# A two-layer graph network on one core: layer 1's mean row out of unused mask columns, norms from LayerNorm's statistics, and a late last column for three tiles

## The chip, the cores and the metric

The kernel runs on one core of one Trainium2 chip. Its time is the device time of one execution in microseconds (us). Three runs of the kernel before gave 1134.03, 1134.79 and 1137.2 us; the median is 1134.79 us.

## The reference

Input: x of 2708 x 256 in fp32 and a sparse 0/1 matrix adj of 2708 x 2708. Two layers follow; each adds a graph attention and then a mixture of experts (top 2) to x. The change concerns the attention of layer 1, cut here to what matters:

```
x = LayerNorm(x)
Wx   = logmap0(x)[:, 1:] @ W_gcn            # logmap0: arccosh(x0) * y / |y|, y = x[:, 1:]
h    = logmap0(proj(expmap0([0, Wx]))) @ W_att
e    = h @ a1 + (h @ a2).T
att  = softmax(where(adj > 0, e, -9e15), axis=1)
emb  = proj(elu(att @ h));   out = expmap0(sigmoid(logmap0(emb)))
```

In a softmax over a row, h @ a1 cancels, so every neighbour j has the weight p_j = exp(h_j . a2), whatever the row: a row's result is the sum of p_j h_j over its neighbours, divided by the sum of p_j. A row without a neighbour gets the plain mean of all rows of h. The maps only scale rows: h_j is a matrix product u_j times a factor that depends on two norms, that of the normalised x_j and that of u_j.

## The kernel before

**Tiles.** Rows lie in T = 22 tiles: 0 to 19 of 128 rows, 20 and 21 of 74 each (TAIL); LAST is 21. D is 256. The order of instructions on TensorE (PE), DVE, ACT and SP is the order in which the program writes them; only POOL's is left to the framework. Each engine works in order.

**Layer 0** (attention, line 1246, and experts) lasts until about 662 us. Then a stage of layer 1 follows, in which a step counter (`Turns`) interleaves pairs of tiles: `prepare1` adds two partial sums (POOL), takes LayerNorm's statistics (DVE, line 434), the root on ACT (lines 441 and 442), and applies it (line 450); `project1` turns the rows (PE), copies them (ACT, line 1571), multiplies with w1x (PE, line 473) and evicts u_ps: ACT squares u with a sum into `norms` (line 1584) and copies u into h_all (line 1586). `square_rows` (line 1458) takes the norm of the normalised x on ACT too. Column 0 of each normalised row goes to `c0` (POOL).

**Factors.** `factors1(lo, n)` works on [128, n] statistics, one column a tile: a root of three blocks of norms (ACT Ln and Exp, lines 1603 and 1604, one Newton step on DVE), log1p as a series (about 20 DVE instructions), the scale of each row, p_all = exp(score) on ACT (line 1613) and p_scale = p_all * scale. It runs for 12 tiles, and after the projections for the other 10. `split_h` then writes p_j h_j of each tile as two fp32r halves, `half0` (ACT, line 1635) and the remainder `half1` (DVE, line 1636), with p_j itself in column D.

**Attention 1.** For a tile i of rows, `sum_up(i, j)` multiplies the mask block of (i, j), widened from fp8 to fp32r, with both halves of tile j: 22 x 2 matmuls of 128x258 (line 1649) sum in one PSUM bank. `widen(i, part)` casts the blocks of even or odd j, 128x1408, on POOL (line 1525) or ACT (line 1527) into one of four buffers. Rows without a neighbour get an artificial one: row 74 of tile LAST holds TINY/N times the sum of all h, at weight TINY. `add_h` makes that sum: 22 fp32 matmuls with scale as the weights (line 1656), from h_all; `split` then writes it into the halves (lines 1635 and 1636). Tiles 0 and 1 are summed first, over j from 0 to FIRST = 12; then come the mean and the rest of their columns; then tiles 2 to 21.

**After a tile**, `finish1`: DVE RECIPROCAL (line 1772), ACT Relu, Exp and Tanh (1775 to 1777), DVE twice (1779, and 1780 which reads PSUM), ACT Square (1784). When the last tile of a group is done (tiles 0 to 5, 6 to 11, 12 to 17, 18 to 21), `points1` of the group starts (line 1824): root and log chains on DVE and ACT, x1, LayerNorm, the logits on PE, `pick`, `rank` on PE, `number` on DVE, and the scatter of the rows to `rows_d` in DRAM, one indirect DMA a tile and choice, issued by POOL (line 681). Experts 1 works on blocks of 128 rows: SP fetches a block from rows_d (line 772) and its weights (lines 756 and 760), PE turns it (tr_ps, line 468), multiplies (lines 887 and 905), DVE weighs. Blocks 0 to 7 are known after groups 0 and 1, blocks 8 to 19 after group 2, the rest after group 3; `bias_ps` (line 858) and `number_ps` (826) belong to that planning.

**The order from tile 2 on** comes from a planner at build time, `Clock`: every piece of work is a generator that yields ("PE", 0.265) and the like, an engine and an assumed time in us, or a `Mark` to wait for; `Slots` are its buffers. It writes the instructions in the order in which the pieces would start. Its times are assumptions; on the chip each engine's queue then runs in that order. `widener` gives casts of tiles below 12 to POOL, later even parts to ACT.

The mask has no use for columns 74 to 127 of tiles 20 and 21: they are set to zero (lines 483 and 484), and the rows of PSUM that they make are not read.

Of the kernel before, what the change touches and what calls it, by code (L numbers as in the profile page):

```python
# [22 lines left out]
P = 128  # L23
# [123 lines left out]
def kernel(  # L147
# [260 lines left out]
    def log1p(u):  # L408

        t = ts(u, 1.0, OP.add)  # L410
        k = ts(t.bitcast(I32), 23, OP.logical_shift_right, dtype=I32)
        down = ts(k, -1.0, OP.mult, 254.0, OP.add, dtype=I32)
        scale = ts(down, 23, OP.logical_shift_left, dtype=I32).bitcast(F32)
        m = tt(tt(u, scale, OP.mult), ts(scale, -1.0, OP.add), OP.add)
        z = tt(m, recip(ts(m, 2.0, OP.add)), OP.mult)
        z2 = tt(z, z, OP.mult)
        terms = [2.0 / (2 * n + 1) for n in range(8)]
        q = ts(z2, terms[7], OP.mult)
        for c in reversed(terms[1:7]):
            q = sts(q, c, OP.add, z2, OP.mult)  # L420
        q = sts(q, terms[0], OP.add, z, OP.mult)
        return tt(ts(k, -127.0, OP.add, math.log(2.0), OP.mult), q, OP.add)

# [996 lines left out]
    ln_a1 = Norm("a1")  # L1420
    norms = kept("norms", 1.0, 2 * T).rearrange("p (k t) -> p k t", k=2)

# [32 lines left out]

    def square_rows(xp, pair):
        for q, (t, r) in enumerate(pair):
            nc.scalar.activation(row_tile("junk", 4)[:r, 1:], xp[q][:r, 1:], AF.Square,
                                 accum_out=norms[:r, 0, t:t + 1])

    def ahead(b):
# [13 lines left out]
        if left == 1:  # L1475
            rsqrt(ts(ln_a1.mv[:, :2 * AHEAD, 1], LN_EPS, OP.add), ln_a1.rstd[:, :2 * AHEAD])
            for k, pair in enumerate(pairs[:AHEAD]):
                keep_rows(h_all[:, 2 * k:2 * k + 2, :D], pair)
                if k < AHEAD - 1:
                    normed[k] = [(xn_tile if k < 2 else xr0_tile)()[:, :D] for _ in pair]  # L1480
                    for xp, (t, r) in zip(normed[k], pair):
                        ln_a1.apply(xp, x_all[:, t], t, r)
        if left == 0:
            for k, pair in enumerate(pairs[:AHEAD - 1]):
                square_rows(normed[k], pair)

# [24 lines left out]
    zeros = filled("zeros", 0.0, T, pool=att)  # L1511
    tiny = filled("tiny", TINY, pool=att)
    nc.scalar.preload_act_table_set(LN_TABLE)
    HALF = T // 2
# [14 lines left out]

    c0, scale, p_all, p_scale = kept("c0", 1.0), kept("scale"), kept("p_all"), kept("p_scale")  # L1530

    def xr_tile():
# [6 lines left out]
    def prepare1(pair):  # L1539

        xa = h_all[:, pair[0][0]:pair[0][0] + 2, :D]
        xb = [xr_tile()[:, :D] for _ in pair]
        fetch_rows(xa, sums0[0], pair)
        for q, (t, r) in enumerate(pair):
            fetch_row(xb[q], sums0[1], t, r)
        yield 3
        for q, (t, r) in enumerate(pair):
            nc.gpsimd.tensor_tensor(xa[:r, q], xa[:r, q], xb[q][:r], OP.add)
        yield 1
        keep_rows(xa, pair)  # L1550
        for q, (t, r) in enumerate(pair):
            ln_a1.stats(xa[:r, q], t, r)
        yield 1
        ln_a1.root(pair)
        yield 1
        ln_a1.mend(pair)
        xp = [xr_tile()[:, :D] for _ in pair]
        for q, (t, r) in enumerate(pair):
            ln_a1.apply(xp[q][:r], xa[:r, q], t, r)
        yield 1  # L1560
        yield from project1(pair, xp)

    def project1(pair, xp):
        ps = ps_tile("tr_ps", "tr").rearrange("p (t c n) -> p t c n", c=DC, n=P)
        for q, (t, r) in enumerate(pair):
            turn_rows(xp[q][:r], r, ps[:, q])
            nc.gpsimd.tensor_copy(c0[:r, t:t + 1], xp[q][:r, 0:1])
        yield 1
# [3 lines left out]
        else:  # L1572
            for q, (t, r) in enumerate(pair):
                nc.scalar.copy(xt[:, q, :, :r], ps[:, q, :, :r])
        if pairs.index(pair) >= AHEAD - 1:
            square_rows(xp, pair)
        yield 1
# [5 lines left out]
        for q, (t, r) in enumerate(pair):  # L1583
            nc.scalar.activation(row_tile("junk", 4)[:r, 1:], us[q][:r, :D - 1], AF.Square,
                                 accum_out=norms[:r, 1, t:t + 1])
            nc.scalar.copy(h_all[:r, t, :], us[q][:r, D - 1:])  # L1586

    def minus(v):

        nc.vector.tensor_scalar(v[..., 1:], v[..., :1].bitcast(F32), -1.0, None, op0=OP.mult)  # L1590

    def factors1(lo, n):

        hi = lo + n


        d = ts(c0[:, lo:hi], -1.0, OP.add, THETA_EPS, OP.max)
        v = stat(3 * n)
        sts(d, 2.0, OP.add, d, OP.mult, v[:, :n])
        nc.vector.tensor_scalar(v[:, n:].rearrange("p (k t) -> p k t", k=2), norms[:, :, lo:hi],  # L1600
                                MIN_NORM * MIN_NORM, None, op0=OP.max)
        y = stat(3 * n)
        nc.scalar.activation(y, v, AF.Ln)
        nc.scalar.activation(y, y, AF.Exp, scale=-0.5)
        yield 1
        y = newton(v, y)
        u = tt(tt(v[:, :n], y[:, :n], OP.mult), d, OP.add)
        f = tt(log1p(u), y[:, n:2 * n], OP.mult)
        wx = tt(tt(v[:, 2 * n:], y[:, 2 * n:], OP.mult), f, OP.mult)
        part = sts(wx, LEAST, OP.max, recip(ts(wx, MIN_NORM, OP.max)), OP.mult)  # L1610
        tt(part, f, OP.mult, scale[:, lo:hi])
        score = tt(scale[:, lo:hi], h_all[:, lo:hi, D], OP.mult)
        nc.scalar.activation(p_all[:, lo:hi], score, AF.Exp)
        yield 1

        tt(p_all[:, lo:hi], scale[:, lo:hi], OP.mult, p_scale[:, lo:hi])
# [25 lines left out]
    def sum_up(i, j):  # L1644
        k = rows_of(j)
        if i not in accs:
            accs[i] = ps_tile("att_ps", "acc")
        for half_k in halves:
            nc.tensor.matmul(accs[i][:, :D + 2], wide_masks[i, j % 2][:k, j // 2, :],  # L1649
                             half_k[:k, j, :], start=(j == 0 and half_k is halves[0]),  # L1650
                             stop=(j == LAST and half_k is halves[1]))

    def add_h(mean, lo, hi):

        for t, r in tiles[lo:hi]:
            nc.tensor.matmul(mean[:96, :D], scale[:r, t:t + 1].to_broadcast([r, 96]),
                             h_all[:r, t, :D], start=t == 0, stop=t == LAST)

    turns = Turns()
    FIRST = 12  # L1660
    last = pairs[AHEAD - 1]
    normed[AHEAD - 1] = [xr_tile()[:, :D] for _ in last]
    for xp, (t, r) in zip(normed[AHEAD - 1], last):
        ln_a1.apply(xp, x_all[:, t], t, r)
    for k in range(AHEAD):
        turns.start(project1(pairs[k], normed[k]), k)
    for k in range(17):
        if AHEAD + k < len(pairs):
            turns.start(prepare1(pairs[AHEAD + k]))
        turns.step()  # L1670
        if 6 <= k < 10:
            widen(k % 2, k < 8)

        if k == FIRST // 2 - AHEAD + 10:
            turns.start(factors1(0, FIRST))
        if k >= 14:
            lo = 4 * (k - 14)
            split_h(lo, lo + 4)
    split_h(lo + 4, FIRST)
    turns.start(factors1(FIRST, T - FIRST))  # L1680
    turns.finish()
    psum_stage(wide=5, acc=3)
    mean = ps_tile("mean_ps")
    for j in range(FIRST):
        for i in range(2):
            sum_up(i, j)
    add_h(mean, 0, T)
    split_h(FIRST, FIRST + 4)
    split_h(FIRST + 4, LAST)
    nc.scalar.preload_act_table_set(TANH_TABLE)  # L1690
    split(LAST, slice(64, 96), mean[64:96, :D], TINY / N)
    split(LAST, slice(0, TAIL), h_all[:TAIL, LAST, :D], p_scale[:TAIL, LAST:])
    for part in range(2):
        for t in range(FIRST + part, T, 2):
            for i in range(2):
                sum_up(i, t)
        widen(2, part)

# [19 lines left out]
    acc_slots = {t: acc.take() for t in range(2)}  # L1718
    wide_slots = {(2, part): wides.take() for part in range(2)}

    wide_at = {(i, part): Mark() for i in range(2, T) for part in range(2)}
    for part in range(2):
        wide_at[2, part].at = 0.0
    started, widened = Mark(), Mark()
# [12 lines left out]
    def widener():  # L1737
        for i in range(3, T):
            for part in range(2):
                wide_slots[i, part] = yield from wides.get()  # L1740
                clock.start(widen_one(i, part, wide_tile()), 0)
# [8 lines left out]
    def attention():  # L1750
        for i in range(2, T):
            acc_slots[i] = yield from acc.get()
            accs[i] = ps_tile("att_ps", "acc")
            for part in range(2):
                yield wide_at[i, part]
                for j in range(part, T, 2):
                    yield "PE", 0.265
                    sum_up(i, j)
                clock.set(wide_slots[i, part])
            clock.start(finish1(*tiles[i]), 0)  # L1760
        att_scope.close()
        late_pools()
        clock.set(started)

    def finish1(t, r):
# [253 lines left out]
    experts1.beside = add_beta  # L2019
    for t in range(2):  # L2020
        clock.start(finish1(*tiles[t]), 0)
    clock.start(widener())
# [55 lines left out]
```

## Time and profile before

| | |
|---|---|
| runs | 1134.03, 1134.79, 1137.2 us (median 1134.79) |
| the profiled execution | 1136.56 us, its span 1134.8 us, granted TensorE clock 0.958 |
| projections of layer 1 | TensorE 662.2 to 708.8 |
| attention 1, tiles 0 and 1, with the mean | 710.4 to 730.6 |
| attention 1, the other tiles | to 862.8 |
| wait before the first block of experts 1 | 867.8 to 880.05 |
| last matmul of experts 1 | about 1094 |

The profile is of one execution, and its times count from the span's start. The span is that of the profiled instructions; what lies around it makes the 1136.56 us. Each line of a timeline has a start, a duration, the engine, the source line, the operation, what it writes and reads, and in brackets the idle time before it with what ended it. Line numbers are those of the kernel before; after `log1p` and further changes, the changed kernel's are 16 to 125 higher.

### The profile page before, as it was taken

The numbers are of one execution on the slowest core, as the hardware profiler recorded it, in microseconds if no ns is written. First come the engines' busy times: TensorE is split into PE (matmuls) and PEld (weight loads), VectorE is DVE, ScalarE is ACT, GpSimd is POOL, SyncE is SP. The second block draws the span as 40 slices with busy tenths as digits, with TensorE's granted clock in tenths as the row PEclk, the third lists the DMA queues.
The fourth block names the chain that finished last, engine by engine and source line by source line (L and its number), as shares of the span: only waits on it lengthen the run. The fifth ranks groups of instructions, "written<-read, shape, count | busy, mean of one in ns | idle before, by whom it ended". The sixth has DMA issues, their size and how long they took to land. (4 is left out here: it accounts for less than half of the span.)

```text
span 1134.8 us, 21254 instructions
## 1 busy us (share of the span) xinstructions
PE 1023.5 (90%) x6665; PEld 909.0 (80%) x6665; DVE 541.9 (48%) x2083; ACT 572.7 (50%) x1599; POOL 367.1 (32%) x417
## 2 busy tenths in 40 slices
PE   5999999998999999999999999998984888999950
PEld 3788888886889999999998853898984787898840
DVE  7778888887420111111111235647777552122368
ACT  4867667664524444444443357536754543444320
POOL 7531112111242222212222350253345166433442
PEclk9999999999989999999999999999897889999985
DMA  9965354431889999999899959400225477787974
GB/s 289 288 242 177 136 175 156 166 95 58 303 251 295 327 326 322 323 306 321 257 311 335 340 160 278 150 1 6 76 84 153 124 215 188 187 213 178 282 194 133
DMA packets 165461, 238.96 MB, mean 211 GB/s; under 512 B 11035, under 2 KB 140374, under 8 KB 162632
## 3 DMA queue, kind: packets, MB, share of 16 engines
q1 hardware_dynamic: 146524, 214.09, 57.9%
q0 software_dynamic: 18816, 23.42, 10.6%
q8 instruction: 56, 0.92, 0.3%
q14 instruction: 65, 0.53, 0.2%
HBM read 205.54 MB, written 54.99 MB: 230 GB/s over the span
## 5 line engine op out<-in xcount | busy, mean ns | idle before, releaser
L911 DVE TENSOR_SCALAR yo<-out_ps,w 128x256 f32<-128x256 f32 x92 | 44.5, 483 | 402.4 <-PE out_ps L905 401.9
L1246 PE MATMUL att_ps<-g_all,z 128*128 128x257 f32 (+3 forms) x968 | 223.6, 383 | 0.0
L905 PE MATMUL out_ps<-room,ht 128*128 128x256 f32 x872 | 201.1, 383 | 0.0
L1246 PEld LDWEIGHTS att_ps<-g_all,z 128*128 128x128 f32 (+3 forms) x968 | 174.9, 186 | 29.6 <-issue 3.1
L887 PEld LDWEIGHTS hid_ps<-xt,room 128*128 128x128 f32 x1504 | 176.4, 193 | 7.3 <-issue 2.5
L887 PE MATMUL hid_ps<-xt,room 128*128 128x128 f32 x1504 | 177.7, 277 | 4.2 <-DMA room<-in_L_ffn_W_dram 3.7
L905 PEld LDWEIGHTS out_ps<-room,ht 128*128 128x128 f32 x872 | 162.7, 192 | 21.3
L1232 ACT ACTIVATE zr<-e_bc,minus_one,g_all 128x256 f32<-128x256 f32 (+3 forms) x242 | 130.4, 591 | 46.4 <-DVE z L1235 45.8
L916 POOL DMA_INDIRECT sums<-yo,xg x43 | 66.8, 1554 | 235.0 <-DVE side L879 173.4
L891 ACT ACTIVATE ht<-hid_ps,w_t 128x128 f32<-128x128 f32 x376 | 128.7, 364 | 28.0 <-PE hid_ps L887 8.8
L681 POOL DMA_INDIRECT rows_d<-xr,place x88 | 92.2, 1048 | 121.0 <-DVE xr L450 76.9
L1649 PE MATMUL att_ps<-half,wide_mask 128*128 128x258 f32 (+1 forms) x968 | 124.5, 290 | 2.5 <-ACT h_all L1586 1.5
L1649 PEld LDWEIGHTS att_ps<-half,wide_mask 128*128 128x128 f32 (+1 forms) x968 | 121.5, 195 | 3.9 <-ACT h_all L1586 2.4
L1235 DVE SCALAR_TENSOR_TENSOR z<-zr,mask_t 128x256 f32<-128x256 f32 (+3 forms) x242 | 96.9, 422 | 29.6 <-ACT zr L1232 18.3
L916 POOL DMA_INDIRECT sums<-yo,xr x45 | 70.6, 1569 | 118.0 <-DMA sums<-yo,xr 30.0
L891 ACT ACTIVATE ht<-hid_ps,w1x 128x128 f32<-128x128 f32 x180 | 62.4, 363 | 88.6 <-PE hid_ps L887 85.0
L881 ACT ACTIVATE w<-xg,side 128x1 f32<-128x1 f32 x43 | 12.7, 294 | 169.2 <-DVE side L879 169.2
L1525 POOL CAST wide_mask<-mask_t 128x1408 fp32r<-128x1408 fp8e4 x31 | 42.5, 1375 | 101.6 <-PE att_ps L1649 67.5
L887 PE MATMUL hid_ps<-lo,wide_mask 128*128 128x128 f32 x480 | 63.4, 287 | 5.6 <-DMA wide_mask<-in_L_ffn_w_dram 4.7
L887 PEld LDWEIGHTS hid_ps<-lo,wide_mask 128*128 128x128 f32 x480 | 60.6, 200 | 9.4 <-issue 6.5
L905 PE MATMUL out_ps<-wide_mask,ht 128*128 128x256 f32 x240 | 59.6, 393 | 0.0
L468 PE MATMUL tr_ps<-ident,xr 128*128 128x128 f32 (+1 forms) x214 | 38.2, 289 | 22.2 <-DMA xr<-rows_d 13.9
(292 smaller groups left out, 1325.0 us busy)
## 6 DMA issues: line engine op xcount, KB each, us to landing
room<-in_L_ffn_W_dram SPq DMA_DIRECT2D x94, 1024.0 KB
wide_mask<-in_L_ffn_w_dram SPq DMA_DIRECT2D x60, 512.0 KB
room<-in_adj_dram SPq DMA_DIRECT2D x20, 1354.0 KB
room<-in_L_ffn_w_dram SPq DMA_DIRECT2D x30, 512.0 KB
rows_d<-nobody SPq DMA_DIRECT2D x1, 7511.0 KB
rows_d<-nobody SPq DMA_DIRECT2D x5, 1295.0 KB
sums<-nobody SPq DMA_DIRECT2D x2, 2944.0 KB
xr<-rows_d SPq DMA_DIRECT2D x45, 129.5 KB
```

What stands on the lines that cost most here:

```text
L468: nc.tensor.transpose(ps[:, c, :r], src[:, c * P:(c + 1) * P], ident[:r, :r])
L681: ins = nc.gpsimd.indirect_dma_start(out=self.rows_d[:, :], in_=self.rows[t][:r], in_offset=None, out_offset=bass.IndirectOffsetOnAxis(ap= ...
L887: nc.tensor.matmul(ps[:, :P], w1_b[:, c, f * P:(f + 1) * P], xt[:, c, :], start=(c == 0), stop=(c == DC - 1))
L891: nc.scalar.activation(ht[:, f, :], ps[:, :P], self.func, bias=self.bias[:, f, b:b + 1])
L905: nc.tensor.matmul(ps[:, :D], ht[:, f, :], self.rooms[b % 3][1][:, f, :], start=False, stop=(f == self.FC - 1))
L911: nc.vector.tensor_scalar(yo, ps[:, :D], w, None, op0=OP.mult)
L916: ins = nc.gpsimd.indirect_dma_start(out=self.sums[k][:, :], in_=yo, in_offset=None, out_offset=bass.IndirectOffsetOnAxis(ap=self.rows.pop ...
L1232: nc.scalar.activation(zr[:k, :n], e_bc[:k, lo:lo + n], AF.Relu, bias=minus_one[:k], scale=g_all[:k, j, D + 1:D + 2])
L1235: nc.vector.scalar_tensor_tensor(z[:k, :n], zr[:k, :n], 1.0, mask_t[:k, j // 2, lo:lo + n, j % 2], op0=OP.add, op1=OP.mult)
L1246: nc.tensor.matmul(accs[i][:r, :D + 1], z[:k, q * P:q * P + r], g_all[:k, j, :D + 1], start=(j == 0), stop=(j == LAST))
L1525: nc.gpsimd.tensor_copy(m, src)
L1649: nc.tensor.matmul(accs[i][:, :D + 2], wide_masks[i, j % 2][:k, j // 2, :], half_k[:k, j, :], start=(j == 0 and half_k is halves[0]), stop ...
```

## The change

1. *Norms from statistics.* `square_rows` goes. `inward1` computes the squared norm of y from LayerNorm's variance, rstd and c0 (D * var * rstd^2 - c0^2), and the factor f of the first map for all 22 tiles at once, in `f_all`. `factors1` keeps the second map alone, for 16 and then 6 tiles. All are generators now, so that single steps can be placed between others; the copies to c0 move ahead of the turning.
2. *First casts.* The four casts for tiles 0 and 1 all go to POOL; two were on ACT.
3. *Order.* inward1 and the first factors run among the last projections, tiles 0 to 2 are split ahead of the last eviction, and two steps of the remaining factors follow each split of tiles 4 to 15.
4. *The mean.* `add_h` goes. Tile 20, now SPARE, is summed first after tiles 0 and 1. Columns 126 and 127 of its widened masks get 1/p_j, in two parts (`spare_columns`, six DVE instructions), so that rows 126 and 127 of its sum hold the sum of all h but that of LAST. ACT copies this sum to SBUF (`keep_total`); in the middle of tile 2's even columns two fp32 matmuls add those two rows and LAST's own part; `split_last` makes the halves of LAST. Only then do tiles 0, 1 and SPARE (OPEN) get their column LAST, between tile 2's even and odd columns, the masks for it kept by three small POOL copies; SPARE's sum is put back by a matmul with the identity, as its bank's sum was closed. Tile 2 sits in a bank of another pool ("wide").
5. *What the planner and the framework make of it.* The order of tiles is 0, 1, 20, 2, 3, ... 19, 21. finish1 of tile 20 moves from the end of the attention to its start. ACT casts (20, even); POOL casts (20, odd) and then those of tiles 2, 3 and so on. Six fetches of x_d for the last group move on SP ahead of one block's fetch and weight load.

The diff, cut to its core (`log1p` and `factors1` get a `yield` after nearly every instruction):

```diff
+    def inward1():
+        n = T
+        rest = tt(sts(ln_a1.mv[:, :, 1], float(D), OP.mult, ln_a1.rstd, OP.mult), ln_a1.rstd, OP.mult)
+        rest = tt(rest, tt(c0, c0, OP.mult), OP.subtract)
...
+        nc.vector.tensor_scalar(v[:, n:], rest, MIN_NORM * MIN_NORM, None, op0=OP.max)
+        y = yield from root_of(v)
...
+        log = yield from log1p(u)
+        yield
+        tt(log, y[:, n:], OP.mult, f_all)
...
         for half_k in halves:
-            nc.tensor.matmul(accs[i][:, :D + 2], wide_masks[i, j % 2][:k, j // 2, :],
+            late = j == LAST and i in OPEN
+            nc.tensor.matmul(accs[i][:, :D + 2],
+                             last_masks[i][:k] if late else wide_masks[i, j % 2][:k, j // 2, :],
...
-    def add_h(mean, lo, hi):
-        for t, r in tiles[lo:hi]:
-            nc.tensor.matmul(mean[:96, :D], scale[:r, t:t + 1].to_broadcast([r, 96]),
-                             h_all[:r, t, :D], start=t == 0, stop=t == LAST)
+    SPARE = TF
+    OPEN, NEXT = (0, 1, SPARE), 2
+    def spare_columns():
+        p_inv = ts(p_all, 1e-30, OP.max)
+        p_inv = recip(p_inv)
+        by_part = p_inv.rearrange("p (j s) -> p s j", s=2)
+        for part in range(2):
+            hi, lo = (wide_masks[SPARE, part][:, :, P - 2 + k] for k in range(2))
+            nc.vector.tensor_copy(hi, by_part[:, part])
+            nc.vector.tensor_tensor(lo, by_part[:, part], hi.bitcast(F32), OP.subtract)
...
-    FIRST = 12
+    FIRST, SOON = 16, 3
...
+        if k == 15:
+            go(near, 1)
+            go(near)
+            split_h(0, SOON)
...
         if 6 <= k < 10:
-            widen(k % 2, k < 8)
+            widen(k % 2, k < 8, pool=True)
...
+    far = factors1(FIRST, T - FIRST)
+    for t in range(SOON, FIRST):
+        split_h(t, t + 1)
+        if t >= SOON + 1:
+            go(far, 2)
+    go(far)
+    split_h(FIRST, LAST)
+    keep_last_masks()
     nc.scalar.preload_act_table_set(TANH_TABLE)
...
     for part in range(2):
-        for t in range(FIRST + part, T, 2):
+        for t in range(FIRST + part, LAST, 2):
             for i in range(2):
                 sum_up(i, t)
-        widen(2, part)
+        widen(SPARE, part)
+    spare_columns()
...
     def attention():
-        for i in range(2, T):
+        for i in order:
...
+                    if i == NEXT and part == 0 and j == 8:
+                        slot = yield from bank.get()
+                        ps = ps_tile("mean_ps")
+                        yield total_at
+                        yield "PE", 0.9
+                        nc.tensor.matmul(ps[:96, :D], two_last, total["tile"][:, :D], start=True, stop=False)
+                        nc.tensor.matmul(ps[:96, :D], scale[:TAIL, LAST:].to_broadcast([TAIL, 96]),
+                                         h_all[:TAIL, LAST, :D], start=False, stop=True)
+                        clock.start(split_last(ps, slot, last_at), 0)
...
+                if i == NEXT and part == 0:
+                    yield last_at
+                    for k in OPEN:
+                        if k == SPARE:
+                            yield "PE", 0.5
+                            nc.tensor.matmul(accs[k][:, :D + 2], ident, total["tile"], start=True,
+                                             stop=False)
+                            clock.set(total["slot"])
+                        yield "PE", 0.265
+                        sum_up(k, LAST)
+                        clock.start(finish1(*tiles[k]), 0)
...
+    def split_last(ps, slot, mark):
+        yield "ACT", 0.4
+        by = TINY / N
+        nc.scalar.activation(halves[0][64:96, LAST, :D], ps[64:96, :D], AF.Copy, scale=by)
+        yield "DVE", 0.5
+        nc.vector.scalar_tensor_tensor(halves[1][64:96, LAST, :D], ps[64:96, :D], by,
...
+        yield "ACT", 0.4
+        lo, by = slice(0, TAIL), p_scale[:TAIL, LAST:]
+        nc.scalar.activation(halves[0][lo, LAST, :D], h_all[lo, LAST, :D], AF.Copy, scale=by)
+        yield "DVE", 0.5
+        nc.vector.scalar_tensor_tensor(halves[1][lo, LAST, :D], h_all[lo, LAST, :D], by,
...
```

The last DVE instruction of `split_last` is at line 1885 of the changed kernel (N1885 in the prediction).

## The prediction

> **What bounds the kernel now.** I read, in this order: the page's first two parts, TensorE's timeline through layer 1's attention, its waits behind it, and then POOL's and DVE's timelines for what those waits hang on.
>
> ```profile
> span 1134.8 us, 21254 instructions
> PE 1023.5 (90%) x6665; PEld 909.0 (80%) x6665; DVE 541.9 (48%) x2083; ACT 572.7 (50%) x1599; POOL 367.1 (32%) x417
> ```
>
> TensorE is busy 90%, but shares say nothing of one stage. The stage of the change, on TensorE's timeline (start, duration, work, and in brackets the idle time before with what ended it):
>
> ```profile
> 706.90 1.94 PE L473 MATMUL u_ps<-w1x,xts 128*74 128x512 f32 x4 [0.91 <-ACT h_all L1586]
> 710.37 6.01 PE L1649 MATMUL att_ps<-half,wide_mask 128*128 128x258 f32 x48 [1.53 <-ACT h_all L1586]
> 716.22 9.91 PE L1656 MATMUL mean_ps<-h_all,scale 128*96 128x256 f32 x44
> 725.78 14.44 PE L1649 MATMUL att_ps<-half,wide_mask 128*128 128x258 f32 x117
> ```
>
> The mean costs 9.9 us of a TensorE that runs without a gap. What the attention leads to is the second thing to see:
>
> ```profile
> 861.76 1.00 PE L1649 MATMUL att_ps<-half,wide_mask 128*128 128x258 f32 x7
> ...
> 865.89 1.87 PE L858 MATMUL bias_ps<-hot_f,w1x 16*128 16x8 f32 x8 [1.98 <-DVE hot_f L850]
> 880.05 0.69 PE L468 MATMUL tr_ps<-ident,xr 128*128 128x128 f32 x2 [12.30 <-DMA xr<-rows_d]
> ```
>
> The attention ends at 862.8, but experts 1 can't begin before 880.05: TensorE waits 12.30 us for rows that POOL scatters and SP fetches again. POOL's timeline (first and last of the twelve scatters of group 1) and SP's queue:
>
> ```profile
> 857.59 0.97 POOL L681 DMA_INDIRECT rows_d<-xr,place  x1 [4.15 <-DVE ended L807]
> ...
> 872.04 0.96 POOL L681 DMA_INDIRECT rows_d<-xr,place  x1 [0.30 <-issue]
> ```
> ```profile
> 877.94 2.59 SPq L772 DMA_DIRECT2D xr<-rows_d  x3
> ```
>
> The scatter waits for DVE, which works through points, pick and places of group 0 and then of group 1 almost without a pause from 789 to 858. That chain begins when group 0's last tile, tile 5, has its finish1:
>
> ```profile
> 755.32 1.01 DVE L1824 TENSOR_SCALAR stat<-emb_sq 128x6 f32<-128x6 f32 x1 [0.58 <-ACT xn L1784]
> ```
>
> So the path to the end is: project phase, tiles 0 to 5, DVE's chain of groups 0 and 1 (755 to 858), twelve scatters, fetch, 880, then the blocks at about 3.84 us each and the last LayerNorm. Work of TensorE between tile 5 and 862 is not on it. **The question is when tile 5 ends, not what TensorE saves.**
>
> **The change part by part.** Times are on the profiled execution's span.
>
> *Project phase.* Twenty-two ACT squares (L1458, 0.40 + 0.19 us each) and two ACT casts (L1527, 1.37 and 1.35 us at 685.8 and 688.8) go. They are behind TensorE's pauses of 0.65 (690.80) and 0.91 us (706.90; there ACT sat in p_all's wait for DVE as well). The pause of 1.53 us at 710.37 holds the eviction of the last tile (0.36 + 0.19 + 0.36) behind split work; alone it is about 0.9, so 0.6 goes, and some 0.25 us at the phase's start, where squares stand ahead of the first eviction. Taken to the upper side of their overlap: 0.65 + 0.91 + 0.6 + 0.25 = 2.4; with the last eviction's first half hidden under the last project, 2.6. I take 2.6, attention at 707.8; ends: 1.6 (the first two alone) and 3.3 (all of the 1.53 too). The new work of the phase, the chain for 22 columns, is 27 DVE instructions at a pitch of 0.205 us, 5.6 us, in a stage where DVE is busy 10 of 20 us: hidden, but p_all must be out before the last tile is evicted; I reckon 703.8 against 706.9, 3 us of cover. POOL's two more casts lie in time it is idle.
>
> *Tiles 0 and 1.* Before: 710.37 to 730.6 for 88 matmuls and the mean. After: 84 matmuls at a pitch of 0.1205 us (5.31 us for 44), but no faster than DVE delivers halves. From about 707.2 DVE has, up to tile 9's half, seven splits at 0.41 and 22 small ones at 0.205 (the row of eleven small ones from 721.98 to 723.41 gives 1.43), 7.4 us, and two trips over ACT, 1.5 together (714.42 to 714.97 and 721.70 to 721.98 in the old chain, with queueing): j=10 starts at 716.1. Then eleven columns at 4 x 0.1205: 716.1 + 5.3 = 721.4. That is 9.2 us ahead of 730.6: 2.6 from the phase, 6.6 of the mean's 9.9.
>
> *Tile SPARE ahead of tile 2.* It needs its casts and the 1/p columns. ACT loads its table (1.28) after the last split, 719.0 to 720.3, and casts (20,0) to 721.85; POOL casts (20,1), (2,0), (2,1) back to back, 720.5 to 724.75. The six small DVE instructions of spare_columns come meanwhile, about 1.2 us if nothing holds them. What can hold them shows in DVE's timeline, beside POOL's:
>
> ```profile
> 732.34 1.43 DVE L1779 SCALAR_TENSOR_TENSOR lo<-xn,lo 128x256 f32<-128x256 f32 x1 [1.20 <-ACT lo L1777]
> ```
> ```profile
> 830.29 4.69 DVE L387 SCALAR_TENSOR_TENSOR stat<-stat,stat 128x6 f32<-128x6 f32 x8
> ```
> ```profile
> 831.89 2.67 POOL L1525 CAST wide_mask<-mask_t 128x1408 fp32r<-128x1408 fp8e4 x2
> ```
>
> The first takes 0.43 us elsewhere (753.80); here it ends with POOL's cast. In the second, eight instructions that need 1.6 take 4.69, across two casts in a row. So SPARE starts at 722.55 (columns done before the cast bites; TensorE idle 1.2), at 723.65 (one instruction slips in at each boundary of casts; idle 2.3) or at 725.2 (held through all three; idle 3.8). The row of 4.69 (one pass of two casts without a gap to slip in) speaks for the later ones, single instructions that did pass between two POOL instructions at 678.8 and 1115.2 for the middle. I take the middle and keep both ends.
>
> The Trainium skill (page "SBUF — State Buffer", section "🔬 SBUF: two separate sides") speaks against the change here: the port pair that VectorE and GpSimd share is an exclusive lock, held for a whole instruction, and the loser blocks. The row of 1.43 agrees. By the rule alone, with POOL always next in line, the sum would be the late end, 725.2; the row of 4.69 has one such case.
>
> *Late columns.* SPARE is 42 matmuls, 5.06 us: end S = 728.7 (727.6, 730.3). Then tile 2: its 44 take 5.31; two fp32 mean matmuls 0.9 (two of the 22 at 0.45); the total put back by an fp32 matmul with 258 columns, 0.46; the six late matmuls 0.72. Between tile 2's part 0 and the late columns TensorE waits for the last half: eviction of the total 0.45, mean, then ACT 0.38, DVE 0.42, ACT 0.51, DVE 0.48 (the rows at 727.19 to 728.61, with 0.5 us of handing over at two of them). I get S + 4.25 for that against S + 3.65 for TensorE, idle 0.65; and 2.0 if the cast of (4,0), which starts as part 0's buffer comes free, holds the last DVE instruction. Tile 2 ends at S + 8.0 or S + 9.3. Before it ended at 735.95 (its RECIPROCAL 736.27).
>
> Sum at tile 2: best 735.55, **-0.4 us**; middle 728.7 + 8.6 = 737.3, **+1.35**; worst 730.3 + 9.25 = 739.55, **+3.6**. From there tiles 3 to 5 are as before, so group 0's chain and the start of experts 1 move by the same: 880.05 becomes about 881.4. That is where the mean's 9.9 us go: 5.3 of tile 20 are moved ahead of group 0, 2.1 are new matmuls, the rest waits.
>
> *Later.* The attention ends about 4 us earlier (tile 20 is done); that lengthens TensorE's wait before 880 and no more. It helps group 3: its points begin about 4 us earlier, and the finish1 of tile 20 (DVE about 1.05 us, ACT about 1.9) is out of the crowded 858 to 863. TensorE's pauses that hang on groups 2 and 3:
>
> ```profile
> 907.62 0.20 PE L826 MATMUL number_ps<-fresh_bf,tri 58*58 58x32 bf16 x1 [3.15 <-DVE fresh_bf L822]
> ...
> 931.61 0.41 PE L468 MATMUL tr_ps<-ident,xr 128*128 128x128 f32 x2 [1.59 <-DMA xr<-rows_d]
> ```
>
> With 0.33, 0.93 and 0.33 between, 6.3 us. Group 2 sits behind block 0 in TensorE's queue and moves with 880, so I count 1.3 of it as gained (mainly the 1.59); ends 0 and 6.3. SP's six fetches of x_d that pass one weight load cost nothing in a queue that stands idle from 870 to 877.9; if that load were needed at once, its own 0.4 to 0.5 us each, 3 in all, would show in the weight waits (8.2 us now). The blocks, 3.84 us each from 938 on, are TensorE's own and hand a shift through.
>
> Sum: +1.35 - 1.3 = 0.05, nothing. The profiled execution was 1136.56 (span 1134.8), 1.8 above the median of 1134.79; the sum is a difference, so I set it on the median: **1134.8 us**.
>
> **The rivals.**
> *Faster: DVE gets through early and groups 2 and 3 gain.* -0.4 at tile 2 and 3 to 6.3 of the later pauses: 1128.1 to 1131.4, say 1130. For it: if tile 20's halves are done by 719, as I reckon, the first of the six instructions stand ahead of the casts; the pauses exist. Against: the row of 4.69.
> *Faster, the mean's time passes through.* If group 1's chain is held by the order of TensorE's queue (rank and number stand among the attention's matmuls) and not by DVE, then a shift of 4 to 8 comes through: 1127 to 1131. Against: DVE has no pause over 1.5 us in 789 to 858, the scatter is released by DVE.
> *Slower: the casts lock DVE out.* Place: spare_columns, and N1885 in the late columns. Held through all three casts and once more: +3.6, nothing later gained, 1138.4; it decides from the point that the first of the six DVE instructions doesn't end before 722.1.
> *It doesn't do what it says:* the far factors, not the mean, set tiles 0 and 1; DVE's trips over ACT take 3 us more than I count and 721.4 becomes 724.4. +3 over the middle, less 1.3: 1137.8 or, with the lock, 1141.
>
> **How the numbers follow.** Chances: no change (middle) 0.42; first faster case 0.24, second 0.08; lock 0.18; far factors 0.08. 0.3% (3.4 us) is about what a measurement of this kernel can tell from no change. Faster 0.32, same 0.42, slower 0.26. Range: from 1128 (the best sum) to 1140 (lock 1138.4 and part of the late factors); left out are the second faster case's lower half and the upper end of the last, with what a new order by the planner may do, about 0.2. Signs are mixed; the middle alone is 1133.4 to 1138.
>
> **What would show it.** Right: attention from 707.8, tiles 0 and 1 done near 721.4, SPARE's first matmul at 722.5 to 725.2, tile 2's RECIPROCAL near 737.6, the first matmul of block 0 near 881.4 after a wait for rows_d longer than 12.30. Wrong: tile 5's finish moved by more than 4 us either way, a scatter of group 1 that begins before 855, or the pauses of 900 to 935 unchanged or grown.

## The result

Over twenty runs each the changed kernel takes 1137.1 us (median) and the kernel before 1135.51; the ratio is 1.0014, with a 95% interval from 0.9999 to 1.0029. Twelve further runs on a chip of the same pace gave 0.9993 (0.9973 to 1.0013). So nothing that can be told from no change, as forecast; 1137.1 lies within 1128 to 1140.

### The profile page after: what moved, and what is told of

Same layout as the page of the kernel before. It is cut to its first block, busy times and chain, and to the rows that moved or that the text cites. A ratio compares the mean times of both kernels' runs of the same rounds, so it can differ in the third digit from the quotient of the medians.

```text
span 1139.4 us, 21113 instructions
## 1 busy us (share of the span) xinstructions
PE 1019.4 (89%) x6627; PEld 905.7 (79%) x6627; DVE 541.5 (48%) x2071; ACT 560.8 (49%) x1555; POOL 371.2 (33%) x425
## 5 line engine op out<-in xcount | busy, mean ns | idle before, releaser
L1262 PE MATMUL att_ps<-g_all,z 128*128 128x257 f32 (+3 forms) x968 | 226.4, 387 | 0.0
L1536 POOL CAST wide_mask<-mask_t 128x1408 fp32r<-128x1408 fp8e4 x34 | 46.4, 1372 | 93.4 <-PE att_ps L1688 93.4
L903 PEld LDWEIGHTS hid_ps<-lo,wide_mask 128*128 128x128 f32 x480 | 60.9, 201 | 8.5 <-issue 4.7
```

The costliest lines, as they stand in the source:

```text
L903: nc.tensor.matmul(ps[:, :P], w1_b[:, c, f * P:(f + 1) * P], xt[:, c, :], start=(c == 0), stop=(c == DC - 1))
L1262: nc.tensor.matmul(accs[i][:r, :D + 1], z[:k, q * P:q * P + r], g_all[:k, j, :D + 1], start=(j == 0), stop=(j == LAST))
L1536: nc.gpsimd.tensor_copy(m, src)
```

## The profile after

The profiled execution took 1141.08 us, 4 above its own median; its page begins:

```profile
span 1139.4 us, 21113 instructions
PE 1019.4 (89%) x6627; PEld 905.7 (79%) x6627; DVE 541.5 (48%) x2071; ACT 560.8 (49%) x1555; POOL 371.2 (33%) x425
```

TensorE has 4 us less work and the span is not shorter. TensorE's timeline through the stage of the change:

```profile
708.44 4.89 PE L1688 MATMUL att_ps<-half,wide_mask 128*128 128x258 f32 x33 [0.82 <-ACT h_all L1600]
713.50 1.42 PE L1688 MATMUL att_ps<-half,wide_mask 128*128 128x258 f32 x8 [0.16 <-DVE half L1674]
715.98 5.53 PE L1688 MATMUL att_ps<-half,wide_mask 128*128 128x258 f32 x43 [1.07 <-DVE half L1674]
723.47 6.50 PE L1688 MATMUL att_ps<-half,wide_mask 128*128 128x258 f32 x52 [1.96 <-DVE wide_mask L1706]
729.81 0.59 PE L1837 MATMUL mean_ps<-xr,two_last 128*96 128x256 f32 x2
```

The solid 9.91 us of the mean are gone. In their place the halves come at DVE's pace (0.16 and 1.07 of waiting), then TensorE waits 1.96 us for DVE's 1/p columns, and SPARE's 42 matmuls stand ahead of tile 2. Further on, TensorE's line for the first block, POOL's first scatter of group 1, and the start of group 0's points on DVE:

```profile
880.81 0.69 PE L484 MATMUL tr_ps<-ident,xr 128*128 128x128 f32 x2 [12.55 <-DMA xr<-rows_d]
```
```profile
858.25 0.98 POOL L697 DMA_INDIRECT rows_d<-xr,place  x1 [5.63 <-DVE ended L823]
```
```profile
755.82 1.01 DVE L1949 TENSOR_SCALAR stat<-emb_sq 128x6 f32<-128x6 f32 x1 [0.58 <-ACT xn L1909]
```

All three stand within 0.8 us of where they stood (755.32, 857.59, 880.05), while the attention ended at 857.8 and not at 862.8. Executions drift by some microseconds in layer 0, so from here on times count from E, the end of layer 0's last expert matmul (661.1 before, 662.2 after). Times by E, from the profiles of these two kernels on chips of the faster kind (see the experiments):

| | before | before_third | after | after_rounds |
|---|---|---|---|---|
| first attention matmul | 49.3 | 49.3 | 46.3 | 46.3 |
| tile 2's RECIPROCAL | 75.2 | 75.2 | 74.9 | 76.3 |
| points of group 0 | 94.2 | 94.2 | 93.7 | 95.0 |
| end of attention | 201.7 | 202.1 | 195.7 | 196.9 |
| first scatter of group 1 | 196.5 | 197.0 | 196.1 | 197.3 |
| first block | 218.9 | 219.6 | 218.6 | 220.1 |

## The experiments

They ran on chips of two kinds: on one kind the kernel before takes 1135 to 1138 us, on the other 1157 to 1159. Ratios are always to the kernel before on the same chip; stages up to the points of group 0 agree between the kinds within 0.05 us where the granted clock was the same. In the texts from before a run, "look" means one execution with its profile, and "rounds" are timed runs of a kernel beside the kernel before.

**1. Both kernels again** (unchanged; slower chip).

> The kernel before once more, for how far the same kernel's stages differ between two executions. Times count from the end of layer 0's last expert matmul (E; 661.1 in the first profile): first attention matmul E+49.3, group 0's points E+94.2, first scatter of group 1 E+196.5, first block E+218.9. If these repeat within 0.5 us, differences of the changed kernel of 0.3 to 0.6 us up to the first block (which it shows) are no more than noise, and the place to look is behind it; the rival is that the stages differ by 1 us and more by themselves, so that a single profile can't tell where 1.6 us of the median come from.

> The changed kernel once more. In its first profile, from the same point E (662.2): first attention matmul E+46.3, group 0's points E+93.7, first scatter of group 1 E+196.1, first block E+218.6; then 58.9 us from block 0's to block 7's weighing (56.2 or less would be as before: 907.6 and 931.6 waits of 3.15 and 1.59, here 4.50 and 2.37). Theory: the stretch up to the first block repeats within 0.5 us, and the longer stretch behind it (+2.3 us) repeats too, because groups 2 and 3 now come no earlier but block 0 to 7 wait longer for them. Rival: the +2.3 us is chance of this execution, and this time the stretch is within 0.7 us of the 48.4 us between block 0 and block 7 of before.

Before repeated to 0.03 us up to the points (E+94.23). After did not: its points stand at E+95.18, 1.5 us later than in its first profile, though SPARE began at the same E+61.3 after the same pause (1.97). The difference is in the 52 matmuls behind it, 7.99 us against 6.50:

```profile
722.92 7.99 PE L1688 MATMUL att_ps<-half,wide_mask 128*128 128x258 f32 x52 [1.97 <-DVE wide_mask L1706]
```

In half-microsecond stretches the granted clock was 0.50 from 724.0 to 727.0 (1.00 all through in the first profile). So up to the points the first expectation held for before and fell for after. Behind the points it fell for before too: the first scatter of group 1 came at E+197.2 (196.5) and the first block at E+227.4 (218.9), with a pause that experiment 8 comes back to. From block 0 to block 7, by TensorE's output matmuls, there were 54.6 us (before_again 55.9), on the faster chips 50.6 in the first profile of after, 48.3 in after_rounds, 48.4 and 48.2 in two of before: the +2.3 of the first profile was chance.

**2. Parts 1 to 3 with the old mean** (slower chip, 12 runs; the mean stands behind 16 columns of tiles 0 and 1).

```diff
-    SPARE = TF
-    OPEN, NEXT = (0, 1, SPARE), 2
...
+    SPARE, OPEN, NEXT = 2, (), -1
...
+    add_h(mean, 0, T)
...
-    spare_columns()
```

> Parts 1 to 3 of the change alone (norms from statistics, casts on POOL, factors for 16 + 6), with the old mean of 22 fp32 matmuls behind the first 16 columns of tiles 0 and 1, and tiles in the old order. Theory: the earlier start of the attention (E+46.3 against 49.3) is lost again, as halves come at DVE's pace (16th column at about E+57), and the mean follows bare: tiles 0 and 1 end at about E+70.3 against 69.5, group 0's points at E+95.0 (before 94.2), first block E+219.7; time 0 to 2 us above before. Rival: the mean still hides the six far columns' factors, and all 2.6 to 3 us of the phase pass: points at E+91.5, first block E+216.2, time 3 us below before.

Ratio 1.0001 (0.9980 to 1.0022). Tile 0 was done at E+69.0 (before 69.6), points at E+93.7: 0.5 us early where the theory had 0.8 late and the rival 2.7 early. The timeline shows the mean bare:

```profile
716.48 3.02 PE L1687 MATMUL att_ps<-half,wide_mask 128*128 128x258 f32 x23 [1.07 <-DVE half L1674]
719.33 9.68 PE L1694 MATMUL mean_ps<-h_all,scale 128*96 128x256 f32 x44
728.66 13.57 PE L1687 MATMUL att_ps<-half,wide_mask 128*128 128x258 f32 x109
```

Of the 3.0 us by which the attention starts earlier, about 2.5 go into waits for DVE's halves: 0.16 and 1.07 in one piece, the rest in pauses too short for a row of their own.

**3. The old kernel without the mean** (slower chip, 10 runs; 21 of the 22 tiles are left out of the mean, so that rows without a neighbour get another value).

```diff
-                             h_all[:r, t, :D], start=t == 0, stop=t == LAST)
+                             h_all[:r, t, :D], start=t == lo, stop=t == LAST)
...
-    add_h(mean, 0, T)
+    add_h(mean, LAST, T)
```

> The kernel before with the mean of tile LAST's rows alone (21 of 22 matmuls of add_h left out; rows without a neighbour get another value). What the mean's removal is worth without the other parts. Theory: the factors of the last 10 tiles come from a DVE chain that ends at E+61 (p_scale at 722.0 in the trace) and their halves after it, so TensorE waits where the mean stood, and tiles 0 and 1 end at about E+67.3, 2.2 us earlier than before and not 8.6 as with the new factors; time 0.2% below before. Rival (the mean itself was the bound of this stage): tiles 0 and 1 end at E+60 to 61.5, time 0.7% below before.

Ratio 1.0025 (1.0002 to 1.0048), and tile 0 done at E+69.63, where before has 69.64: not 2.2 us earlier but none. TensorE's timeline:

```profile
715.54 6.02 PE L1649 MATMUL att_ps<-half,wide_mask 128*128 128x258 f32 x48 [1.53 <-ACT h_all L1586]
726.76 1.14 PE L1656 MATMUL mean_ps<-h_all,scale 74*96 74x256 f32 x2 [5.21 <-issue]
727.92 0.58 PE L1649 MATMUL att_ps<-half,wide_mask 128*128 128x258 f32 x1
729.13 11.07 PE L1649 MATMUL att_ps<-half,wide_mask 128*128 128x258 f32 x73 [0.63 <-DVE half L1636]
```

Where the mean stood, TensorE stands and waits for the factors of the last ten tiles: DVE writes their p_scale at E+60.9 with the mean and without it. **In the kernel before, leaving out the mean's 9.9 us gains nothing: most of them filled a wait for DVE.** Not all, for the theory had 2.2 us left over. What the trace shows for those is the clock. Behind the pause of 5.21 us it was granted at half (the first row below, in the columns explained further down), and TensorE, without a gap from 729.13 on, took about 0.215 us a matmul where it takes 0.12 at the full clock, some 2 us for the 21 up to 733.7:

```profile
729.13:733.70 4.57, 4.57 (x21) 4.57 (x22) 3.53 (x9) 4.05 (x9) 0.00 (x0) 0.50 0.00 0
733.70:735.90 2.20, 2.20 (x20) 2.20 (x20) 1.58 (x1) 1.31 (x2) 1.36 (x1) 0.99 0.00 0
```

In the kernel before, the clock is 1.00 all through this stage. No run shows what leaving out the mean is worth at the full clock.

**4. The new factors without the mean** (slower chip, 6 runs; the same work left out).

```diff
-    add_h(mean, 0, T)          # as in experiment 2
+    add_h(mean, LAST, T)
```

> As the run with the old mean, but with the mean of tile LAST's rows alone (one tile of 22 is summed; rows without a neighbour get another value): what the change would be worth if the mean cost nothing and no tile were moved ahead. Theory (DVE's chain of groups 0 and 1 sets the first block, and hands on what tile 5 gains one to one): tiles 0 and 1 end at E+60.9, group 0's points at E+85.6, first block at about E+210.3, 8.6 us ahead of before, time 5 to 9 us below before. Rival (the first block hangs on the place of group 1's rank and number in the queue of TensorE, or on POOL, not on tile 5): the points are 8 us early and the first block less than 4 us.

Ratio 0.9927 (0.9899 to 0.9955). Tile 0 done at E+60.98, points at E+85.56, both as written, 8.7 us early; first scatter of group 1 5.9 and first block 7.3 us ahead of before_again, where the theory had 8.6. The points, with E at 665.14:

```profile
750.70 1.01 DVE L1933 TENSOR_SCALAR stat<-emb_sq 128x6 f32<-128x6 f32 x1 [0.58 <-ACT xn L1893]
```

At the points, parts 1 to 3 are worth 0.5 us alone, the mean's removal 0.0 alone, and both together 8.7. Most of what tile 5 gains comes through; both kernels have the pause of experiment 8 on the way here, 10.1 us before and 6.8 in this run, so how much comes through is read from experiment 7.

**5. The 1/p columns off DVE** (slower chip, 6 runs). **6. Tile 2's casts on ACT** (one run on a slower chip, then 11 on a faster one).

```diff
         p_inv = recip(p_inv)
+        pieces = [stat(T, F32R) for _ in range(2)]     # 5: DVE ahead of the casts, ACT copies
+        nc.vector.tensor_copy(pieces[0], p_inv)
+        nc.vector.tensor_tensor(pieces[1], p_inv, pieces[0].bitcast(F32), OP.subtract)
...
+                nc.scalar.copy(wide_masks[SPARE, part][:, :, P - 2 + k],
...
-        pool = part or i < POOL_WIDENS                 # 6
+        pool = (part or i < POOL_WIDENS) and i != NEXT
```

> The changed kernel with the 1/p columns made otherwise: DVE writes both parts to two [128,22] tiles ahead of the casts, ACT copies them into the masks (four copies of 128x11). Theory (POOL's casts hold DVE's instructions, 1.27 and 1.39 us in the trace where 0.2 are needed): SPARE starts about 1.1 us earlier after the end of tiles 0 and 1 (idle 0.9 where it was 1.96), group 0's points at E+92.6 instead of 93.7, time 0.1% below the changed kernel, which its total can't tell. Rival (the pause before SPARE comes from its casts, not from the columns): the idle stays at 1.7 to 2.0.

> The changed kernel with the two casts of tile 2 on ACT instead of POOL, nothing else. The cast of SPARE's odd part stays on POOL. Theory of the held port: with no POOL cast beside them, the columns' subtraction and second copy take about 0.2 us each instead of 1.27 and 1.39, and SPARE starts at about E+60.3 instead of 61.3, idle about 1.0. Rival: these instructions are slow by their form (11 elements with a stride, fp32r out), and take 1.2 us and more beside ACT's casts too.

> The changed kernel with tile 2's casts on ACT, in rounds. Its look had SPARE's start 1.1 us earlier than the changed kernel, and group 0's points at E+92.6. Theory: the held port is worth 1.1 us and no more, so the ratio to before is 0.998 to 1.000 (points at E+92.6 where before has 94.2, first block about E+217.5): it can't mend the change, since tile 20's 5.1 us and 1.9 us of added matmuls still stand ahead of group 0. Rival (the lock was the main loss): ratio below 0.996.

DVE's timeline of after, and POOL's beside it:

```profile
722.06 1.27 DVE L1706 TENSOR_TENSOR wide_mask<-stat,wide_mask 128x11 fp32r<-128x11 f32 x1
723.25 1.39 DVE L1705 CAST wide_mask<-stat 128x11 fp32r<-128x11 f32 x1
724.67 0.18 DVE L1706 TENSOR_TENSOR wide_mask<-stat,wide_mask 128x11 fp32r<-128x11 f32 x1
```
```profile
720.63 3.98 POOL L1536 CAST wide_mask<-mask_t 128x1408 fp32r<-128x1408 fp8e4 x3 [27.94 <-PE att_ps L1688]
```

The same two instructions of act_casts_rounds, where ACT casts beside them and POOL doesn't:

```profile
719.86 0.18 DVE L1706 TENSOR_TENSOR wide_mask<-stat,wide_mask 128x11 fp32r<-128x11 f32 x1
719.95 0.17 DVE L1705 CAST wide_mask<-stat 128x11 fp32r<-128x11 f32 x1
```

1.27 and 1.39 become 0.18 and 0.17: it is POOL's cast, not the form. TensorE's pause before SPARE falls to 0.62 in act_columns and 0.88 in act_casts_rounds:

```profile
728.97 6.51 PE L1688 MATMUL att_ps<-half,wide_mask 128*128 128x258 f32 x52 [0.62 <-ACT wide_mask L1707]
```
```profile
720.19 6.48 PE L1688 MATMUL att_ps<-half,wide_mask 128*128 128x258 f32 x52 [0.88 <-DVE wide_mask L1705]
```

Points at E+92.3 and E+92.6, first block in act_casts_rounds at E+218.5 (expected 217.5). Its ratio on the faster chip is 0.9999 (0.9975 to 1.0023), as the theory had it. On the slower chip act_columns has 0.9942 (0.9922 to 0.9962). That need not be the columns: the one run of after_again, with the changed kernel as it is, took 1150.83 us on such a chip, where the kernel before has a median of 1156.83 and no run under 1153.4 (see experiment 8).

**7. The mean from half 0** (6 runs on each kind of chip). Parts 1 to 3 and the old order of tiles; the mean by one fp32r matmul a tile, from what the attention has anyway. It is rounded to one fp32r pass.

```diff
         nc.scalar.activation(p_all[:, lo:hi], score, AF.Exp)
+        nc.scalar.activation(p_inv[:, lo:hi], score, AF.Exp, scale=-1.0)
...
+            if t < LAST:
+                nc.tensor.matmul(mean[:96, :D], p_inv[:r, t:t + 1].to_broadcast([r, 96]),
+                                 halves[0][:r, t, :D], start=t == 0, stop=False)
```

> The changed kernel without its fourth part (no SPARE, no late columns, old order of tiles), with the mean made in another way: for each of 21 tiles one fp32r matmul of half 0 with 1/p_j (one more Exp on ACT a group of factors) as weights, 128x256, put behind that tile's columns of tiles 0 and 1, and LAST's own rows by one fp32 matmul. The mean is rounded to one fp32r pass; nothing is left out. Theory (the mean's replacement ate the gain, as tile 20 and 2.1 us of matmuls stand ahead of group 0): sixteen of the small matmuls lie in TensorE's waits for DVE, tiles 0 and 1 end at about E+61.7 (E is the end of layer 0's last expert matmul; before 69.5), group 0's points at E+86.3 (before 94.2, changed kernel 93.7), and the time is 0.5 to 0.7% below before. Rival (a gain ahead of group 0 is given back behind the first block, in waits for groups 2 and 3): the points are 8 us early but the time is within 0.3% of before.

> The kernel with the mean from half 0 and the new factors, once more, for a chip without the pause that the kernel before shows on the slower one (there the ratio was 0.9914, both with a pause). Theory (a gain ahead of tile 5 is handed on one to one): points of group 0 at E+86.0, first block at E+210.5 to 211.5 where before has 218.9, and the ratio to before 0.992 to 0.994. Rival (the gain on the slower chip came from the pause's place): first block later than E+215, ratio above 0.997.

Ratios 0.9914 (0.9896 to 0.9932) and 0.9926 (0.9899 to 0.9953); 1129.25 us on the faster chip. It beats both kernels, with a mean of lower precision. The theory had 0.5 to 0.7% on the slower chip, where 0.9% came. TensorE's timeline on the faster chip (r_mean_again), by the end of the first sixteen columns:

```profile
717.53 0.28 PE L1697 MATMUL mean_ps<-half,p_inv 128*96 128x256 f32 x1
717.64 0.64 PE L1689 MATMUL att_ps<-half,wide_mask 128*128 128x258 f32 x4
718.12 0.86 PE L1697 MATMUL mean_ps<-half,p_inv 128*96 128x256 f32 x6
718.82 0.59 PE L1700 MATMUL mean_ps<-h_all,scale 74*96 74x256 f32 x2
719.07 12.15 PE L1689 MATMUL att_ps<-half,wide_mask 128*128 128x258 f32 x97
...
872.72 0.69 PE L484 MATMUL tr_ps<-ident,xr 128*128 128x128 f32 x2 [13.00 <-DMA xr<-rows_d]
```

A small matmul takes its place at a pitch of about 0.12 us between the columns (717.53 to 717.64). Twenty-one of them are 2.5 us of TensorE, yet tile 0 is done only 0.2 us later than in experiment 4, which has none: they lie in time that TensorE otherwise waits. Tile 0 is done at E+61.2, points at E+85.95 (8.3 ahead of before_third), first scatter of group 1 at E+188.7 (8.3), first block at E+211.85 (7.75; the theory had 210.5 to 211.5), end 9.8 ahead: about one to one, as the theory said.

**8. The changed kernel in rounds, the kernel before a third time** (faster chip).

> The changed kernel, timed in rounds on the chip of the experiments, where the kernel before takes 1157 us and not 1135.5: there its profile shows DVE and ACT standing for 10 to 11 us at the end of the attention (DVE at the RECIPROCAL of tile 21, released by nothing that the profile names), and the first block at E+227.4 where the first profile had 218.9; the changed kernel's look has no such pause and E+224.6. Theory: the pause belongs to the old order of tiles on this chip, so the changed kernel is 0.3 to 0.6% below before here, without a gain of its own in the attention. Rival: the pause is chance of one execution, the ratio is 1.000 to 1.003 as in the twenty runs.

> The kernel before, a third profile. If the pause of DVE and ACT of some 10 us at the end of the attention stands here again at the same instructions, it goes with this kernel on this chip; if it is gone (first block at E+219), it comes and goes by execution.

These fell on a chip of the faster kind, so they can't tell what happens on the slower. Ratio 0.9993; no pause of DVE in either. On the slower chips it stood at the RECIPROCAL of tile 21 in all five profiles of kernels with the old order of tiles (6.8 to 10.1 us), and in none of three with SPARE ahead. From before_again's DVE:

```profile
878.58 0.17 DVE L1772 RECIPROCAL inv<-att_ps 74x2 f32<-74x2 f32 x1 [10.13 <-remote]
```

In these profiles that goes with the order of tiles and with the chip; the trace names no cause, and it stays open. It is why ratios of the two kinds of chip must not be put side by side. On the slower kind the changed kernel may so be faster by about 0.5%, but for that kernel itself only the one run of after_again says so.

## Why the prediction was right

*The path.* "The question is when tile 5 ends, not what TensorE saves": shown by experiments 4 and 7, where 8.3 to 8.7 us at tile 5 gave 7.3 to 7.9 at the first block and 0.7 to 0.9% of the time, and by after itself, where an attention 6.0 us shorter by E gave nothing. The second faster case (the chain held by TensorE's queue) is thereby out. One reading against that case was wrong: DVE does have pauses over 1.5 us in 789 to 858, of 1.69 and 1.84, and is busy for 53.8 of these 69 us.

*The phase.* 2.6 us were counted, 3.0 measured, the 0.82 us before the attention being the bare eviction that I had put at 0.9.

*Tiles 0 and 1.* Their last matmul, on the scale of the first profile, at 720.5 (forecast 721.4): TensorE went on with j=10 at 714.9 where 716.1 was reckoned. Eleven of the 22 small DVE instructions ahead of it take 0.13 each, as the row of 1.43 says that the prediction cites, and not 0.205. But the step that split the gain into "2.6 from the phase, 6.6 of the mean's 9.9" credits it wrongly. Experiments 2 to 4 show that neither part has it alone: leaving out the old mean gained nothing as long as the factors came late.

*SPARE and the port.* The middle case happened as described: one DVE instruction at each boundary of casts. TensorE waited 1.96 us (forecast 2.3 in that case). On the scale of the first profile SPARE began at 722.4, ahead even of the early end of 722.55, since tiles 0 and 1 ended 0.9 earlier than forecast. The Trainium skill (page "SBUF — State Buffer", section "🔬 SBUF: two separate sides"), by which the loser blocks for the whole of the other's instruction, agrees with 1.27 and 1.39 beside 0.18 and 0.17; its late end, 725.2, did not come, since each instruction got its turn when a cast ended. The lock's price, 1.1 us of pause, is too small to be the change's main loss.

*The sum at tile 2.* Forecast +1.35 (ends -0.4 and +3.6). Measured by E: -0.3, +1.2 and +1.1 in the profiles of after, after_again and after_rounds. Tiles 0 and 1, but for their last column, were 10.1 us ahead of before, and all of that was gone here: 1.96 of pause, 5.06 of tile 20, the added matmuls and small waits. Two things partly cancelled: SPARE started 1.2 us earlier than forecast, and in two of three profiles the clock took about 1.4 back, which the prediction did not have. That these two came out near +1.35 is luck. after_rounds, first the matmuls behind the pause, then two stretches (start and end, length, busy time and instructions of TensorE, its weight loads, DVE, ACT and POOL, then the granted clock):

```profile
718.28 5.92 PE L1688 MATMUL att_ps<-half,wide_mask 128*128 128x258 f32 x36 [1.96 <-DVE wide_mask L1706]
```
```profile
718.60:722.00 3.40, 3.40 (x20) 3.40 (x20) 1.02 (x2) 0.00 (x0) 0.81 (x1) 0.60 0.02 7
722.00:726.00 4.00, 4.00 (x36) 4.00 (x35) 0.00 (x0) 0.38 (x1) 2.31 (x2) 1.00 0.00 0
```

Twenty matmuls in 3.4 us at a mean clock of 0.60, then 36 in 4.0 at 1.00; in half-microsecond stretches the clock is 0.50 from 718.3 to 721.3. Behind the shorter pauses of experiments 5 and 6 (0.62 and twice 0.88) the 52 matmuls took 6.5 us. The Trainium skill (page "TensorE: Matmul & The Clock Gate", section "🔬 Part 1: The HAM clock gate (the "warmup" mystery)") has the clock halved after an idle window of about 3.4 us, by a window that runs freely; the half and the 3.4 us agree with this trace, but here a pause of 1.96 was enough in two executions of three. What spared the third isn't shown.

*Later.* This step failed: "I count 1.3 of it as gained". Nothing was. The attention ended 5 to 6 us earlier by E, yet the points of group 3 began only 0.5 to 1.4 us earlier, without an idle DVE ahead of them: DVE's queue and not the attention holds them. TensorE's waits in the stretch in fact grew:

```profile
908.12 0.23 PE L842 MATMUL number_ps<-fresh_bf,tri 58*58 58x32 bf16 x1 [4.50 <-DVE fresh_bf L838]
...
933.37 0.43 PE L484 MATMUL tr_ps<-ident,xr 128*128 128x128 f32 x2 [2.37 <-DMA xr<-rows_d]
```

The first is 4.50 in all three profiles of after and 3.15 before, and it ended at about the same time by E (246 in the first two profiles): TensorE only came to it earlier. The second is 2.37 and, in after_rounds, 1.80, where before has 1.59 and 1.41. (Of the small pauses that were counted between them, one of 0.33 lies behind both, at 938.59.) Grown pauses here are one of the signs of being wrong that the prediction names, and for this term it was. So the sum is +1.1 at tile 2 in the commoner case, with nothing taken off later: 1135.9 to 1136.6 on either median of before, beside 1137.1. At the points it was -0.55, +0.95 and +0.8 in the same three profiles, and at the first block -0.3 and +0.5 in the two pairs of the faster kind, so nothing is left that a measurement here can tell from no change. That the whole came out at nothing is right in its path and partly luck in its terms: a gain of 1.3 that wasn't there stands against a SPARE that began 1.2 earlier.

*Rivals.* The first faster case had its place right (SPARE began early, and tile 2 was at -0.3 in one profile of three), but the later pauses gave nothing. The lock case needed the first of the six DVE instructions late and three casts held through; the first ended at 720.0. The late factors didn't happen.

## What to carry to other kernels

A busy engine may be filling a wait: the mean looked like 9.9 us of TensorE on the path and was worth 0.0 when it was left out, 8.7 us once the wait behind it was mended too. Take both away before pricing either, and look at the granted clock behind the pause that is left: some 2 of those us went into a halved clock. And work that comes "for nothing" out of unused columns still has a place in the order: tile 20 was not extra work, but 5.1 us of it moved ahead of the tile that sets the end, and a cheap matmul in existing gaps did better.

## What the runs showed of the hardware

A pause of 1.96 us cost TensorE half its clock for about 3.4 us in two of three executions, 1.4 us of time; a pause of 5.21 us was followed by the half clock too, until 7 us after the pause had ended; pauses of 0.62 to 0.88 us, in three profiles, cost nothing beyond themselves. Adding a wait of 2 us to a dense stretch of matmuls can so cost nearly twice the wait. Two small VectorE instructions took 1.27 and 1.39 us beside three GpSimd casts that took 3.98 in a row, and 0.18 and 0.17 without them. One chip kind took 2% longer for the same program, with a pause of 7 to 10 us that, in eight profiles, came with one order of the work and not with the other; its cause is open.
